# Two graph-attention layers on one core: the second group's score row through TensorE, and other places for steps of the prologue

## The chip, the core and the metric

The kernel runs on one core of a Trainium2 chip. The metric is the device time of one execution in microseconds (us), lower is better. Everything is 32-bit floating point, apart from the integer adjacency matrix.

The engines have short names in the profile: PE is TensorE's matrix multiply and PEld its weight load, DVE is VectorE, ACT is ScalarE, POOL is GpSimd, SP is SyncE, which here issues all DMA transfers.

## What is computed

`x` is 64 x 256 x 512 (64 graphs of 256 nodes), `adj` a 256 x 256 matrix of 0 and 1. Two layers follow each other, each with a layer norm and a ReLU ahead of it and a residual addition behind it:

```python
# layer 0: graph attention, W is 512 x 256
h = relu(layernorm(x)) @ W
e = leaky_relu(h @ a[0] + transpose(h @ a[1]), 0.2)      # 256 x 256 for each graph
out = softmax(where(adj, e, -1e9)) @ h
x = x + concat([out, h])
# layer 1: multi-head attention, 8 heads of 64, masked by adj
h = relu(layernorm(x))
q, k, v = h @ Wq.T + bq, h @ Wk.T + bk, h @ Wv.T + bv
x = x + softmax(where(adj, q @ k.T / 8, -inf)) @ v @ Wo.T + bo
```

## The kernel before

The 64 graphs are taken in 32 groups `g` of two graphs `b`; a graph has two tiles `t` of 128 nodes, so a group has four row tiles. The work of a group is written as Python generators, each cut into pieces by `yield`, and a hand-written order of letters says which piece comes when:

- `first_norm(g)` (letter n) is the layer norm ahead of layer 0. `measure(b)` takes statistics on VectorE, GpSimd makes the factor with a power, `norm(b)` writes `xn` on ScalarE, `turn(b)` transposes 32 x 32 blocks on VectorE into `xt` and sends them out (`passed<-xt`), `fetch(b)` brings them back with their blocks in other places (`moved<-passed`, four transfers), and `put(b)` copies them to the operand `hT0` on ScalarE. For the group 0 the turning is done on TensorE instead (`pt`).
- `first_layer(g)` (letter s; for the groups 0 and 1 in the prologue also 0 and 1) makes the features `H = ph`, the attention `e` and the sums `po`. The scores h @ a[0] and h @ a[1] are the first two columns of H. One of them must lie along a row in all partitions: that is the score row, `own`.
- `project(g)` (letter u in the prologue) makes q, k and v of layer 1 in seven products each (Strassen's scheme: sums of quarters of the operands and of the weights, in the order 1, 2, 6, 7, 5, 4, 3). The accumulator of the first product stays in a held bank of PSUM, and ScalarE copies intermediate states to `kept_q`, `kept_k`, `kept_v`. The seventh product of k in the group 0 uses the bank that q's first product held, so it has to wait for q's last copy (`q<-pq`) on ScalarE. From the group 2 on the features are made in the same way (`first_products`).
- `judge()` (letter c) and `mask()` (letter e) make, in the prologue only, bounds on the inputs and the transposed mask: `gram_q`, `gram_k`, then `square_q` and `square_k` in two rounds.
- `weight_sums(name)` makes four sums of the quarters of one weight matrix, on VectorE or GpSimd; `first_weight_sums()` does so for W (GpSimd); `last_bias()` multiplies bv into Wo (`bv_rows`, `pb`).
- `scores(g, b)` (letter S) makes `sc` and the exponentials `p`; `mask_pairs` (m) masks p on VectorE and adds halves on GpSimd; `fold` (f) sends p out (`rows<-p`) and back (`parts<-rows`), adds on GpSimd, and sums on VectorE (`compact<-parts`), which gives the softmax's denominators; `weigh` makes `pr` and `oT`, and `outputs` (o) makes `py`.

Score rows are made in two ways. For the group 0 TensorE transposes a broadcast column of H into PSUM (`pn`). For the others `score_rows(g)` transposes H's first columns on VectorE (`rows<-H`), writes a row of 2 KB to DRAM (`line<-rows`) and reads it back into all partitions (`own<-line`).

A scheduler sets the order of the instructions on each engine from the program's order and the dependencies. Where the kernel wants an order of its own it adds a dependency without a semaphore: `after(instruction, name)`, and `not_sooner(engine, ...)` for "not ahead of the last one that was recorded for this engine". TensorE is pinned throughout (`in_order`). Each engine works through its stream in order, and so does SyncE with the issues of transfers. The lists `put_last`, `norm_last` and others hold names of instructions that later ones are pinned behind.

Buffers that matter here: `xt`, `e` and `r` are single; `parts` of graph 0 takes the buffer of `e`, `own` that of `r`; `xn` and `moved` are double; `kept` is threefold; five banks of PSUM rotate (`mm`), three are held. The prologue of the kernel before ends with these lines (i counts the pieces of `project(0)` from 4 to 20):

```python
    take(*"uunuu0011cc")
    order = "nnn ssn n s - s ss ss s s n - n s - s -".split()
    for i, parts in enumerate(order, 4):
        next(products)
        ...
```

In the profile nearly all TensorE instructions have the line L137 (the helper that pins them; transposes L140) and the other engines' L35 (the helper that remembers the last instruction), so they are told apart by their tiles.

Of the kernel before, what the change touches and what calls it, by code (L numbers as in the profile page):

```python
# [57 lines left out]
def bounded(  # L58
# [56 lines left out]
    def after(instruction, name):  # L115

        tc.add_manual_dep(
            instruction.ins, name,
            mybir.DependencyInfo(mybir.DependencyClass.NoSync, mybir.DependencyReason.DATA),
            reason="the engine's order",  # L120
        )

    def not_sooner(engine, operation, *args, **kwargs):

        last = engine.last
        after(getattr(engine, operation)(*args, **kwargs), last)
# [126 lines left out]
    def weight_sums(name, engine=vector):  # L253
        w = w_sb[name]
        not_sooner(engine, "tensor_sub", w[:, :, T3, :], w[:, :, W22, :], w[:, :, W12, :])
        engine.tensor_sub(w[:, :, T1, :], w[:, :, W12, :], w[:, :, W11, :])
        engine.tensor_sub(w[:, :, T2, :], w[:, :, W22, :], w[:, :, T1, :])
        engine.tensor_sub(w[:, :, T4, :], w[:, :, W21, :], w[:, :, T2, :])
# [8 lines left out]
        not_sooner(gpsimd, "tensor_sub", t2, w22, w12)  # L267
        not_sooner(gpsimd, "tensor_sub", t4, w21, t2)

    put_last, norm_last, edge_last, sums_last, turn_last = [], [], [], [], []  # L270

    def last_bias():

# [346 lines left out]

    def score_rows(g):
        rows = small.tile([P, GT, 8], F32, tag="rows", name=f"rows_{g}", bufs=2)
        not_sooner(vector, "transpose", rows.rearrange("p t c -> p (t c)"), H[:, :, 0:8])
        line = dram.tile([P // 8, S], F32, tag="line", name=f"line_{g}")
        not_sooner(sync, "dma_start", line, rows.rearrange("p t c -> p (t c)")[::8, :])
        own = att.tile([P, P // S, GT, S], F32, tag="r", name=f"own_{g}", bufs=1)
        not_sooner(
            sync, "dma_start", own.rearrange("p k t j -> p (k t j)"),
            line.rearrange("(o k) j -> o (k j)", o=1).to_broadcast([P, TOK]),
        )  # L630
        return own.rearrange("p k t j -> p t k j")
# [64 lines left out]
    def first_layer(g):  # L696
# [38 lines left out]
        pT = {}  # L735
        if g > 1:
            own = owns.pop(g)
            yield
        elif g:
            own = score_rows(g)  # L740
            yield
        else:
            yield
            pn = mm(f"pn_{g}")
            for t in range(GT):
                transpose(pn[:, t * P : (t + 1) * P], H[:, t, 0:1].to_broadcast([P, P]), ident)
            own = pn.rearrange("p (t k j) -> p t k j", t=GT, j=S)
# [103 lines left out]
    def projection(g, name, ops):  # L851
        shape = [P, NT, D] if name == "v" else [P, HP, N]
        turn[0] = 1 - turn[0]
        firsts = 2 if (g, name) == (0, "k") else turn[0]
        sevenths = 1 - turn[0]

        def blocks(bank):
            return bank.rearrange("p (o n) -> p o n", o=2)

        def product(out, i, start):  # L860
            a, w = ops[i][0], w_sb[name][:, :, ops[i][1], :]
            for o in range(2):
                cols = slice(o * P, (o + 1) * P)
                for c in range(2):
                    of, by = (a[:, c, cols], w[:, c, :]) if name == "v" else (w[:, c, cols], a[:, c, :])
                    matmul(
                        out[:, o, :], of, by, start=start and o == c == 0, stop=o == c == 1,
                        skip_group_check=True,
                    )

        def part(b, half):
            if (name, g, b) not in qkv:
                qkv[name, g, b] = place(shape, f"{name}_{g}_{b}")
            to = qkv[name, g, b][0]
            if name == "v":
                return to[:, :, half * D // 2 : (half + 1) * D // 2]
            return to[:, 2 * half : 2 * half + 2, :]

        def take(to, bank, half):

            behind = [scalar.last] if g == 0 and name != "v" else []
            if name == "v":
                taken = [scalar.copy(to, bank)]
            else:
                taken = [
                    scalar.activation(
                        to[:, o, :], bank[:, o, :], AF.Identity,
                        bias=bcol[name][:, 2 * half + o : 2 * half + o + 1], scale=1.0,
                    )
                    for o in range(2)  # L890
                ]
            for last in behind:
                for instruction in taken:
                    after(instruction, last)

        def kept(bank, half, i):
            s = att.tile([P, 2, N], F32, tag="kept", name=f"kept{i}_{name}_{g}", bufs=3)
            take(s, bank, half)
            return s

        first = blocks(held_bank(firsts, f"p{name}1_{g}"))
        product(first, 1, True)
        p1 = kept(first, 0, 0)
        yield
        second = blocks(mm(f"p{name}2_{g}"))
        product(second, 2, True)
        vector.tensor_add(part(0, 0), second, p1)
        yield
        product(first, 6, False)
        p16 = kept(first, 0, 1)  # L910
        yield
        second = blocks(held_bank(sevenths, f"p{name}7_{g}"))
        product(second, 7, True)
        p7 = kept(second, 1, 2)
        yield
        product(first, 5, False)
        vector.tensor_add(part(1, 1), first, p7)
        yield
        product(second, 4, False)
        vector.tensor_add(part(1, 0), second, p16)  # L920
        yield
        product(first, 3, False)
        take(part(0, 1), first, 1)
        yield

# [54 lines left out]
    def fold(g, b, p):  # L980

        if g == NG - 1:
            return
        compact = small.tile([P, NQ, N // S], F32, tag="compact", name=f"compact_{g}_{b}", bufs=2)
        row_sums[g, b] = compact
        pool, tag, bufs = (att, "e", 1) if b == 0 else (big, "hT0", 2)
        rows = []

        def put(quad):
            rows.append(dram.tile([P, QH, N], F32, tag="rows", name=f"rows_{g}_{b}_{quad}"))
            heads = slice(quad * QH, (quad + 1) * QH)
            not_sooner(sync, "dma_start", rows[quad], p[:, heads, 0, :])

        def fetch(quad):
            parts = pool.tile([P, P // S, N], F32, tag=tag, name=f"parts_{g}_{b}_{quad}", bufs=bufs)
            for j in range(QH):
                not_sooner(
                    sync, "dma_start", parts[j * S : (j + 1) * S],  # L1000
                    rows[quad][:, j, :].rearrange("(i a) n -> a i n", a=S),
                )
            return parts

        def add(parts):
            not_sooner(gpsimd, "tensor_add", parts[:, :2], parts[:, :2], parts[:, 2:])
            not_sooner(gpsimd, "tensor_add", parts[:, 0], parts[:, 0], parts[:, 1])

        def sum_up(quad, parts):
            not_sooner(vector, "transpose", parts[:, 1], parts[:, 0])  # L1010
            vector.reduce_sum(
                compact[:, quad], parts[:, 1].rearrange("p (k a) -> p k a", a=S), axis=AX.X
            )

        put(0)
        parts = fetch(0)
        yield
        put(1)
        yield
        add(parts)  # L1020
        yield
        sum_up(0, parts)
        parts = fetch(1)
        yield
        add(parts)
        yield
        sum_up(1, parts)
        vector.reciprocal(compact, compact)
        yield
# [103 lines left out]
    def take(*names):  # L1133
        for name in names:
            next(work[name])
# [10 lines left out]
    take(*"n00c0n0n")  # L1146
    late_loads()
    weight_sums("q")
    take(*"uunuu0011cc")
    order = "nnn ssn n s - s ss ss s s n - n s - s -".split()  # L1150
    for i, parts in enumerate(order, 4):
        next(products)
        if i == 4:
            take("c")
        if i == 17:
            weight_sums("o", gpsimd)
        if i in (5, 12):
            weight_sums("kv"[i // 12])
        if i == 8 and NG > 3:
            load(3, 0)  # L1160
            load(3, 1)
        if i == 11:
            take(*"cc")
        if i == 7:
            first_weight_sums()
        for part in parts:
            if part != "-":
                next(norms if part == "n" else pieces, None)
        if i in (15, 19, 20):
            next(bias)  # L1170
    additions = (piece for g in range(NG) for piece in residual(g))

# [428 lines left out]
```

## Time and profile before

| | before |
|---|---|
| median of 3 runs | 2406.9 us (2406.54 to 2407.69) |
| the profiled execution: time | 2408.41 us |
| the profiled execution: span from first to last instruction | 2406.8 us |
| granted TensorE clock, mean over the span | 0.997 |
| instructions in the profile | 43080 |
| DMA traffic | 343.76 MB, mean 143 GB/s |

The page gives for each engine the time in which it was busy and its share of the span, then groups of instructions, written as what they write, an arrow to the left, and what they read (`ph<-w_sb,hT`), with a count and a mean duration. A timeline lists instructions in order of time: start, duration, engine, line, operation, tiles, shapes, count, and in brackets the idle time ahead of the instruction with what ended it. A 32-bit matmul appears as two records. A granted clock of 1.00 means TensorE at full speed.

### The profile page before, as it was taken

What the parts mean: (1) busy time and instruction counts of PE and PEld (TensorE: products, weight loads), DVE (VectorE), ACT (ScalarE), POOL (GpSimd) and SP (SyncE); (2) the same over time, 40 slices, a digit from 0 to 9 for tenths busy, and PEclk for the clock granted to TensorE, in tenths of its full rate; (3) what the DMA queues carried; (4) which work ended last, traced back from release to release, by engine and by line L of the source; (5) the groups of instructions that cost most, each with busy time, mean ns of one, the idle gap of its engine ahead of it and who ended that gap; (6) DMA issues with size and microseconds to landing.
All of it is one profiled execution on the core that took longest, in us unless ns stands there. A gap on an engine that the chain in (4) does not pass through costs nothing.

```text
span 2406.8 us, 43080 instructions
## 1 busy us (share of the span) xinstructions
PE 2386.7 (99%) x15824; PEld 2014.5 (84%) x15824; DVE 1687.7 (70%) x3346; ACT 1020.9 (42%) x2017; POOL 1420.4 (59%) x1290
## 2 busy tenths in 40 slices
PE   9899999999999999999999999999999999999999
PEld 8778888888888888888888888888888888888886
DVE  7576766777766767667767677776677676676665
ACT  4444444444444444434444444444344444343431
POOL 4456657566666556575556666565655566656552
PEclk9999999999999999999999999999999999999999
DMA  6344444544454444455444444444554445454331
GB/s 194 105 127 145 137 154 149 157 152 134 139 160 149 148 142 138 152 151 166 147 138 134 156 149 148 149 141 142 155 165 145 136 136 163 147 157 141 112 106 46
DMA packets 272041, 343.76 MB, mean 143 GB/s; under 512 B 25424, under 2 KB 217168, under 8 KB 271824
## 3 DMA queue, kind: packets, MB, share of 16 engines
q1 hardware_dynamic: 271824, 340.95, 45.5%
q8 instruction: 126, 2.06, 0.4%
q14 instruction: 91, 0.75, 0.1%
HBM read 177.22 MB, written 163.64 MB: 142 GB/s over the span
## 4 chain that ended last, share of the span: by engine, by line
PE 97%; DMA 1%; DVE 1%; ACT 0%; SPq 0%; issue 0%; POOL 0%; DVEq 0%; ACTq 0%
PE pq L137 16%; PE pk L137 16%; PE py L137 16%; PE pv L137 16%; PE sc L137 10%; PE pr L137 9%; PE ph L137 8%; PE po L137 5%; DMA adj_i<-in_adj_dram 0%; DMA wv_sb<-in_L_gnn_Wv_dram 0%; DMA line<-rows 0%; ACT e L35 0%; PE total L137 0%; PE gram_q L137 0%; PE gram_k L137 0%
## 5 line engine op out<-in xcount | busy, mean ns | idle before, releaser
L35 POOL TENSOR_TENSOR p<-p 128x512 f32<-128x512 f32 x248 | 384.5, 1563 | 490.0 <-DVE p L35 470.4
L35 ACT ACTIVATE xn<-x,factor 128x512 f32<-128x512 f32 x256 | 194.7, 807 | 328.2 <-POOL factor L35 319.3
L35 DVE TENSOR_TENSOR p<-p,maskT 128x1024 f32<-128x1024 f32 x254 | 323.4, 1294 | 2.0 <-ACT p L35 2.0
L35 DVE TENSOR_TENSOR x<-py,x 128x256 f32<-128x256 f32 x448 | 185.9, 415 | 192.8 <-PE py L137 186.5
L35 ACT ACTIVATE p<-sc 128x512 f32<-128x512 f32 x512 | 258.3, 627 | 144.0 <-PE sc L137 127.3
L35 POOL TENSOR_TENSOR parts<-parts 128x512 f32<-128x512 f32 x248 | 248.1, 1001 | 83.0 <-DMA parts<-rows 56.8
L137 PE MATMUL py<-wo_sb,oT 128*128 128x256 f32 x1024 | 262.4, 379 | 0.6 <-DVE oT L35 0.6
L137 PE MATMUL sc<-q,k 64*128 64x256 f32 x2048 | 253.5, 392 | 4.9 <-ACT p L35 4.9
L137 PEld LDWEIGHTS sc<-q,k 64*128 64x128 f32 x2048 | 205.9, 188 | 53.0 <-issue 26.3
L137 PE MATMUL pk<-hT,wk_sb 128*128 128x256 f32 x1024 | 245.6, 383 | 2.8 <-ACT q L35 2.8
L137 PE MATMUL pq<-hT,wq_sb 128*128 128x256 f32 x1024 | 240.0, 382 | 0.7 <-ACT hT L35 0.7
L137 PE MATMUL pv<-wv_sb,hT 128*128 128x256 f32 x1024 | 236.8, 379 | 0.0
L137 PE MATMUL pr<-p,v 128*32 128x256 f32 x4096 | 234.2, 380 | 0.0
L137 PEld LDWEIGHTS pq<-hT,wq_sb 128*128 128x128 f32 x1024 | 191.9, 190 | 36.0 <-issue 10.3
L137 PEld LDWEIGHTS pk<-hT,wk_sb 128*128 128x128 f32 x1024 | 189.9, 190 | 36.6 <-issue 9.9
L35 POOL TENSOR_TENSOR factor<-factor,rexp 128x2 f32<-128x2 f32 (+1 forms) x132 | 117.8, 892 | 171.4 <-DVE factor L35 171.1
L137 PEld LDWEIGHTS py<-wo_sb,oT 128*128 128x128 f32 x1024 | 194.2, 190 | 28.2 <-DVE oT L35 1.1
L137 PEld LDWEIGHTS pv<-wv_sb,hT 128*128 128x128 f32 x1024 | 194.6, 190 | 26.5
L137 PEld LDWEIGHTS pr<-p,v 128*32 128x32 f32 x4096 | 126.8, 110 | 97.8 <-issue 16.9
L137 PE MATMUL py<-wo_sb,o_sums 128*128 128x256 f32 x768 | 197.6, 380 | 0.5 <-DVE x L35 0.5
L137 PE MATMUL pv<-wv_sb,sums 128*128 128x256 f32 x768 | 181.6, 379 | 0.5 <-ACT kept_v L35 0.5
L137 PE MATMUL pk<-sums,wk_sb 128*128 128x256 f32 x768 | 181.5, 379 | 0.0
(150 smaller groups left out, 4076.2 us busy)
## 6 DMA issues: line engine op xcount, KB each, us to landing
passed<-xt SPq DMA_DIRECT2D x124, 512.0 KB, 3.1
moved<-passed SPq DMA_DIRECT2D x496, 128.0 KB, 3.4
rows<-p SPq DMA_DIRECT2D x124, 512.0 KB, 3.4
parts<-rows SPq DMA_DIRECT2D x496, 128.0 KB, 2.9
x<-in_x_dram SPq DMA_DIRECT2D x64, 512.0 KB, 4.3
out_dram<-x SPq DMA_DIRECT2D x62, 512.0 KB, 4.0
own<-line SPq DMA_DIRECT2D x31, 256.0 KB, 3.1
wq_sb<-in_L_gnn_Wq_dram SPq DMA_DIRECT2D x2, 512.0 KB, 9.1
```

Source lines behind the costliest of these rows:

```text
L35: instruction = getattr(self.engine, operation)(*args, **kwargs)
L137: in_order(nc.tensor.matmul(*args, **kwargs))
```

## The change

- The group 1 takes its score row as the group 0 does: TensorE transposes into `pn`, and `score_rows(1)`, with its VectorE transpose and its two transfers, is gone.
- The order of pieces in the prologue is another: the last operand copy of the group 1 (`hT0`) is taken ahead of the loop; the group 1's features, scores and products `po` come earlier among q's products; the third group's second norm and turn follow its first; the second round of squares comes at i = 6; the sums of wv come at i = 11 instead of 12, those of wo at i = 13 instead of 17, those of W after the pieces of i = 6 instead of ahead of those of i = 7; the bias begins at i = 12 instead of 15.
- In `take`, the copies of the group 1's q are pinned behind the last operand copy (`put_last`).
- In `score_rows(2)`, the transpose is pinned behind the last reduction of the fold (`fold_last`, a new list that `sum_up` sets).

```diff
-    put_last, norm_last, edge_last, sums_last, turn_last = [], [], [], [], []
+    put_last, norm_last, edge_last, sums_last, turn_last, fold_last = [], [], [], [], [], []
...
     def score_rows(g):
         rows = small.tile([P, GT, 8], F32, tag="rows", name=f"rows_{g}", bufs=2)
-        not_sooner(vector, "transpose", rows.rearrange("p t c -> p (t c)"), H[:, :, 0:8])
+        last = vector.last
+        turned = vector.transpose(rows.rearrange("p t c -> p (t c)"), H[:, :, 0:8])
+        for other in [last, *fold_last] if g == 2 else [last]:
+            after(turned, other)
...
         if g > 1:
             own = owns.pop(g)
-            yield
-        elif g:
-            own = score_rows(g)
             yield
         else:
             yield
...
             behind = [scalar.last] if g == 0 and name != "v" else []
+            if (g, name) == (1, "q"):
+                behind = list(put_last)
...
                 compact[:, quad], parts[:, 1].rearrange("p (k a) -> p k a", a=S), axis=AX.X
             )
+            fold_last[:] = [vector.last]
...
-    take(*"uunuu0011cc")
-    order = "nnn ssn n s - s ss ss s s n - n s - s -".split()
+    take(*"uunuu0011cccn")
+    order = "nn nsss nsn ssn ss - s s - - - - s - s - -".split()
     for i, parts in enumerate(order, 4):
         next(products)
-        if i == 4:
-            take("c")
-        if i == 17:
+        if i == 13:
             weight_sums("o", gpsimd)
-        if i in (5, 12):
-            weight_sums("kv"[i // 12])
+        if i in (5, 11):
+            weight_sums("kv"[i // 11])
         if i == 8 and NG > 3:
             load(3, 0)
             load(3, 1)
-        if i == 11:
-            take(*"cc")
-        if i == 7:
-            first_weight_sums()
         for part in parts:
             if part != "-":
                 next(norms if part == "n" else pieces, None)
-        if i in (15, 19, 20):
+        if i == 6:
+            take(*"cc")
+            first_weight_sums()
+        if i in (12, 19, 20):
             next(bias)
```

## The prediction

> **What bounds the kernel now.** I read the page first, then the windows over the first 180 us, then the waits of TensorE, then the timelines of TensorE, SyncE and VectorE around each long wait. The engine shares name the bound:
>
> ```profile
> PE 2386.7 (99%) x15824; PEld 2014.5 (84%) x15824; DVE 1687.7 (70%) x3346; ACT 1020.9 (42%) x2017; POOL 1420.4 (59%) x1290
> ```
>
> TensorE is idle for 20.1 of 2406.8 us. The windows (columns: length, busy time of PE, PEld, DVE, ACT, POOL, granted clock, DMA share, GB/s) show that this idle time lies in the prologue, and that the clock falls there too:
>
> ```profile
> 30.00:60.00 30.00, 28.59 (x151) 25.02 (x150) 21.93 (x48) 15.36 (x32) 16.03 (x22) 1.00 0.57 168
> 60.00:90.00 30.00, 26.63 (x119) 21.99 (x118) 21.51 (x42) 13.82 (x29) 8.24 (x8) 0.94 0.31 103
> 90.00:120.00 30.00, 27.15 (x159) 24.34 (x158) 12.47 (x18) 12.43 (x28) 20.73 (x16) 0.94 0.35 109
> 120.00:150.00 30.00, 25.10 (x167) 19.75 (x167) 20.10 (x39) 12.12 (x24) 14.39 (x13) 0.89 0.24 78
> 150.00:180.00 30.00, 30.00 (x201) 24.88 (x200) 23.98 (x48) 13.94 (x24) 20.07 (x20) 1.00 0.63 178
> ```
>
> From 150 us until close to the end TensorE has no gap, so a microsecond saved before 150 should arrive at the end whole. The waits of TensorE name three long ones:
>
> ```profile
> PE sc L137 <- ACT p L35: 4.9, 1, 4.9
> PE ph L137 <- POOL sums_xn L35: 2.8, 1, 2.8
> PE pk L137 <- ACT q L35: 2.8, 1, 2.8
> ```
>
> Each costs twice. In TensorE's timeline (start, duration, what) eight pq/pk records follow each other every 1.73 us, but the ones behind a long wait are stretched:
>
> ```profile
> 58.67 1.89 PE L137 MATMUL pk<-sums,wk_sb 128*128 128x256 f32 x8
> 63.38 2.71 PE L137 MATMUL pk<-hT,wk_sb 128*128 128x256 f32 x8 [2.83 <-ACT q L35]
> 65.88 2.91 PE L137 MATMUL po<-H,e 128*128 128x257 f32 x8
> 68.63 1.89 PE L137 MATMUL pk<-sums,wk_sb 128*128 128x256 f32 x8
> ```
>
> The pk at 63.38 wants q's held bank. Its take stands on ScalarE behind e of the second group (59.51), which waits for own<-line: rows at 54.09, line at 54.33, own at 56.07, landed at 59.5. The last wait has a queue as its cause. VectorE had the third group's rows ready at 118.47, but SyncE stood at the parts transfer, which waits for the fold's reduction (123.32 to 123.74), and only then issued the line (VectorE's timeline, then SyncE's):
>
> ```profile
> 118.26 0.21 DVE L35 STREAM_TRANSPOSE rows<-H 128x32 f32<-128x32 f32 x1
> ...
> 123.32 0.42 DVE L35 TENSOR_REDUCE compact<-parts 128x8 f32<-128x256 f32 x1
> ```
>
> ```profile
> 123.81 1.74 SPq L35 DMA_DIRECT2D parts<-rows  x4
> 125.59 0.54 SPq L35 DMA_DIRECT2D line<-rows  x1
> 128.43 0.35 SPq L35 DMA_DIRECT2D own<-line  x1
> ```
>
> **What the Trainium skill says.** "TensorE: Matmul & The Clock Gate", Part 1, says that the array falls to half clock after about 3.4 us idle, in a free-running window, and needs as long of work to come back. The trace agrees in kind: clock 0.67 in 63.4 to 68.6, 0.54 in 112.3 to 116, 0.57 in 135.6 to 140.3, each after a wait of 2.8 to 4.9 us; after waits of 0.5 to 0.7 us it stays 1.00. [...] here the 2 KB line takes 2.2 us in the median and own 3.4. "GPSIMD Engine Reference", Key points, says that GpSimd shares SBUF interfaces with VectorE, with contention where VectorE has two SBUF inputs; here a p mask takes 1.18 us alone and 2.30 beside GpSimd at 100.87. I keep such stretches at their measured length.
>
> **Stage A, up to the first sc (91.46 before).** *Removed:* one VectorE transpose (0.21), two SyncE issues (0.58 and 0.36), the 5.4 us from rows to own. *Added:* four transposes pn. The first group's took from 19.26 to 20.04, 0.78 us with the wait for the last H copy; the four of pt_mask without it 0.47. I take 0.78, bounds 0.45 to 1.0; TensorE runs in order, so four more instructions can't be a gain.
> - ScalarE now copies the squares and hT before kept_q. The second half of moved is issued at 43.01 to 44.7 and lands within 3.1 us, 47.4; hT's first copy ends at 48.0, ahead of TensorE's own time 49.06. ph starts there instead of 49.90: gain 0.84. kept_q, now behind hT, is wanted by VectorE only near 59.
> - ScalarE then has kept_q, kept_q, two xn of the third group (GpSimd's factor is ready at 50.56, so 50.6 to 52.1) and the H copies (to 53.1). pn ends near 53.3, and e runs 53.4 to 55.0 instead of 59.51 to 61.2.
> - VectorE: both leaky steps to 55.8, a q addition to 56.4, two xt transposes to 57.8 (1.29), masks at 58.5 and 59.2. TensorE meanwhile has pq 1.73, the squares 0.89 + 0.89, pq 1.73 and reaches po at 58.55: just no wait. The squares moved here are the cover; without them po would wait about 1.8 us.
> - q's take follows the third pq (62.2 to 63.0); pk wants it at 65.5. The wait of 2.98 us (60.40 to 63.38 by cadence) goes, and with it the slow stretch (5.25 us from 63.38 to 68.63 instead of 3.46): 1.79.
> - The moved second norm and turn take two ACTIVATE (1.52), two transposes (1.29) and one 512 KB transfer. On SyncE it passes the two x loads of the fourth group, which now wait until about 64.7 instead of 57.7; they land near 72 and are first read near 110. The single xt buffer makes the next transposes wait for the transfer (3.3 us): at worst some 0.4 us at the last pk. The two xn no longer stand between the kept_v copies (80.84 and 84.61), so pv's waits go (0.67 + 0.19 + 0.2 small ones): about 1.0.
> - Weight sums: those of wo and w0 keep their place in GpSimd's stream, those of wv are only split around a k addition. Nothing, covered by the pv products' 3.5 us head start on the third sum.
>
> Sum of A: 0.84 + 2.98 + 1.79 + 1.0 - 0.78 = **5.8 us**; first sc near 85.6.
>
> **Stage B, ph of the third group** (times from the first sc). The pin puts hT's copies ahead of the third kept_q. Before: hT's second copy ended at 18.1 and GpSimd's sums began at 18.2. Now the copies run 10.2 to 12.5 (transfer landed by 8.7), but GpSimd is still in the p additions until 16.5. So sums_xn is ready at 19.1 instead of 20.8, and hT's difference at 20.4. The price: kept_q ends at 13.3, and pq wanted it at 12.58, a new wait of 0.7. ph then waits 0.45 and 0.34. All three are short, so the clock should hold. The stretch from the first ph (107.50) to pk (118.52) was 11.02 us; its work is 6.2, so 4.8 were lost; 1.5 to 1.7 stay. Gain **3.1**: pk at 23.9 instead of 27.06.
>
> **Stage C, e and sc of the second half.** Now the fold's reduction stands ahead of rows. GpSimd's parts additions end near 23.9, the reduction at 24.9, rows at 25.6. SyncE issues four parts (1.74) and line at 26.7; own at 29.2, landed at 32.6 (before 40.5). Two more chains end at e: the second fold (GpSimd 29.9 to 31.9, VectorE to 33.0) and ScalarE's xn and kept_k (33.0). e starts at 33.0, and p 3.0 us later as before (131.94 to 134.94). TensorE reaches sc at 34.4, fills three banks by 35.6 and waits for p until 36.6: 1.0 instead of 4.9, too short to slow the clock. From pk to the next pk<-sums (118.52 to 140.33) it was 21.8 us; now 15.4. Gain **6.4**.
>
> **Sum.** 5.8 + 3.1 + 6.4 = 15.3. VectorE then follows TensorE about 2 us closer than before; py's second read of x had some 2.4 us of slack there. Cost 0 to 1.5, I take 0.8: **14.5 us**. The profiled execution took 2408.41 (span 2406.8), 1.5 above the median of 2406.9. From its own time the sum gives 2393.9, from the median 2392.4; I forecast the latter.
>
> **Rivals.**
> - *e is still late in stage C* (12%): three chains meet within 0.4 us; if one slips by 2 us, the wait is 3 again and the slow stretch of about 2.1 us returns. Gain 10 to 10.5: 2396.6. For it: the fold and own now cross the same SyncE queue. Against it: each piece has its measured length.
> - *Only the e wait of stage A goes* (8%): GpSimd sets stage B and SyncE sets stage C, and the pinned kept_q eats what is left. Gain 5 to 6: 2401.2.
> - *Slower* (3%): the main loop no longer absorbs VectorE's closer following. TensorE has no idle time over 30 groups of about 75 us; if each later group waited 0.65 us at py or po, 30 x 0.65 = 19.5 outweighs the gain and gives about 2412. It decides from 0.48 us a group. Against it: VectorE is idle 19 to 23 us in each such 75 us.
> - *The reorder does nothing* (2%): 2406.9. Against it: pn and the moved squares do stand in TensorE's stream.
>
> **The numbers.** 75% for the sum, with its bounds 2389.5 to 2396; the first rival reaches 2399. Range 2389.5 to 2399.0. About 0.2% (4.8 us) is what a measurement of this kernel can tell. Faster 0.93 (sum, first rival, nearly all of the second), within 0.04, slower 0.03.
>
> **What would show it.** In the new profile: pn near 52.5 with about 0.8 us; e of the second group near 53.5; no long wait before pk; clock 1.00 in the three windows; a wait of about 0.7 at pq and under 0.5 at ph; line issued right after parts, about 27 us after the first sc; sc waiting about 1 us; first sc near 85.6. A wait over 2.5 us anywhere before 150, or idle TensorE after it, proves me wrong.

## The result: 0.54% faster, and the profile after

The median of five runs is 2394.47 us (2394.21 to 2394.69), beside 2407.53 (2406.54 to 2408.81) for five runs of the kernel before: a ratio of 0.9946, 95% interval 0.9931 to 0.9960. The profiled execution took 2394.69, with a span of 2393.0 and a mean granted clock of 1.000. The forecast was 2392.4 with a range of 2389.5 to 2399.0: right in direction and within its range, 2.1 too low.

The page's engine shares first. TensorE is now idle for 2393.0 - 2381.7 = 11.3 us, beside 20.1 before, while its busy time fell too, by 5.0, mostly because the stretched records behind the three long waits are gone:

```profile
PE 2381.7 (100%) x15828; PEld 2010.1 (84%) x15828; DVE 1691.4 (71%) x3345; ACT 1021.8 (43%) x2017; POOL 1422.4 (59%) x1290
```

The windows (length, busy time of PE, PEld, DVE, ACT, POOL, granted clock, DMA share, GB/s): the clock stands at 1.00 in all of them, and TensorE is busy for about 10 us more between 60 and 150:

```profile
60.00:90.00 30.00, 30.00 (x152) 25.64 (x152) 21.56 (x42) 12.85 (x25) 7.73 (x8) 1.00 0.43 146
90.00:120.00 30.00, 29.03 (x204) 24.57 (x206) 13.64 (x25) 13.74 (x32) 27.75 (x23) 1.00 0.36 113
120.00:150.00 30.00, 29.52 (x158) 25.11 (x151) 26.45 (x58) 12.80 (x23) 15.45 (x16) 1.00 0.40 118
```

The waits of TensorE (total, count, longest): the pk wait has left the list, ph fell from 2.8 to 0.6, sc from 4.9 to 0.5, and the pinned kept_q has come in:

```profile
PE ph L137 <- POOL sums_xn L35: 0.6, 1, 0.6
PE py L137 <- DVE x L35: 0.5, 2, 0.3
PE sc L137 <- ACT p L35: 0.5, 1, 0.5
PE pq L137 <- ACT kept_q L35: 0.3, 1, 0.3
```

TensorE's timeline in stage A. The four pn take 0.79 up to the next pq (53.50), po and pk have no bracket, so they waited for nothing, and pk is back at 1.89 a record group, where it was 2.71 before:

```profile
52.71 0.95 PE L140 MATMUL pn<-ident,H 128*128 128x128 f32 x4
53.50 1.89 PE L137 MATMUL pq<-sums,wq_sb 128*128 128x256 f32 x8
...
58.84 2.00 PE L137 MATMUL po<-H,e 128*128 128x257 f32 x8
...
65.87 1.89 PE L137 MATMUL pk<-hT,wk_sb 128*128 128x256 f32 x8
```

The same view in stages B and C, from the first sc at 85.82 on: three waits, all short.

```profile
98.91 1.99 PE L137 MATMUL pq<-hT,wq_sb 128*128 128x256 f32 x8 [0.34 <-ACT kept_q L35]
...
104.98 1.16 PE L137 MATMUL ph<-w_more,sums_xn 128*128 128x129 f32 x8 [0.57 <-POOL sums_xn L35]
...
122.54 2.85 PE L137 MATMUL sc<-q,k 64*128 64x256 f32 x22 [0.48 <-ACT p L35]
```

SyncE's timeline: parts and line still follow each other at once, but 26.8 us after the first sc instead of 34.1.

```profile
110.83 1.73 SPq L35 DMA_DIRECT2D parts<-rows  x4
112.60 0.54 SPq L35 DMA_DIRECT2D line<-rows  x1
115.42 0.34 SPq L35 DMA_DIRECT2D own<-line  x1
```

For the rest I use a table of four marks, read from TensorE's timeline of each profile and counted from the first pq (32.44 before, 32.61 after), because the first 33 us scatter between executions by up to 1 us. *sc* is the first sc (end of stage A), *pk* the first pk of the third group (end of B), *pk2* the next pk<-sums behind the wait for e (end of C), *py* the last py.

| kernel | sc | pk | pk2 | py | median of its runs |
|---|---|---|---|---|---|
| before | 59.02 | 86.08 | 107.89 | 2368.40 | 2407.53 |
| after | 53.21 | 77.29 | 92.71 | 2353.66 | 2394.47 |
| after, second profile | 53.21 | 77.28 | 92.74 | 2353.64 | 2395.07 |
| without the q pin | 53.21 | 77.28 | 92.71 | 2353.42 | 2394.03 |
| without both pins | 53.28 | 77.38 | 96.29 | 2356.72 | 2397.65 |
| row by DMA | 57.84 | 82.05 | 97.41 | 2357.84 | 2398.76 |
| squares late | 55.72 | 79.73 | 94.92 | 2355.52 | 2396.60 |
| before + both pins | 57.37 | 81.43 | 97.16 | 2357.83 | 2398.89 |
| before + second pin | 58.81 | 84.57 | 106.44 | 2367.31 | 2408.45 |
| before + pn | 55.28 | 82.66 | 105.19 | 2365.85 | 2406.83 |
| sums at old places | 53.20 | 77.29 | 92.96 | 2353.64 | 2395.76 |
| half addition on VectorE | 53.21 | 76.51 | 94.97 | 2356.07 | 2397.36 |

The gains by stage are then 5.81 in A, 2.98 in B (24.08 from sc to pk instead of 27.06) and 6.39 in C (15.42 instead of 21.81), 15.18 in all.

### The profile page after: what moved, and what is told of

It is laid out like the page before. It is cut to its first block, busy times and chain, and to the rows that moved or that the text cites. A ratio compares the mean times of both kernels' runs of the same rounds, so it can differ in the third digit from the quotient of the medians.

```text
span 2393.0 us, 43082 instructions
## 1 busy us (share of the span) xinstructions
PE 2381.7 (100%) x15828; PEld 2010.1 (84%) x15828; DVE 1691.4 (71%) x3345; ACT 1021.8 (43%) x2017; POOL 1422.4 (59%) x1290
## 4 chain that ended last, share of the span: by engine, by line
PE 98%; DMA 1%; DVE 0%; ACT 0%; issue 0%; POOL 0%; SPq 0%; ACTq 0%; POOLq 0%; DVEq 0%
PE pq L137 16%; PE pv L137 16%; PE pk L137 16%; PE py L137 16%; PE sc L137 10%; PE pr L137 9%; PE ph L137 8%; PE po L137 5%; DMA adj_i<-in_adj_dram 0%; DMA wv_sb<-in_L_gnn_Wv_dram 0%; PE total L137 0%; PE gram_q L137 0%; PE gram_k L137 0%; ACT hT L35 0%; DMA parts<-rows 0%
## 5 line engine op out<-in xcount | busy, mean ns | idle before, releaser
L35 DVE TENSOR_TENSOR p<-p,maskT 128x1024 f32<-128x1024 f32 x254 | 328.4, 1313 | 3.2 <-ACT p L35 3.2
```

What stands on the lines that cost most here:

```text
L35: instruction = getattr(self.engine, operation)(*args, **kwargs)
```

## The experiments

Beside the experiments, 9 to 17 runs of the kernel before were taken on the same chip; their medians were 2409.30, 2408.49 and 2408.82.

### The score row: does pn carry stage A?

```diff
         if g > 1:
             own = owns.pop(g)
             yield
+        elif g:
+            own = score_rows(g)
+            yield
```

> The changed kernel, with the second group's score row made as before the change (VectorE transpose, row written out and read back) instead of four TensorE transposes. Theory (the row through TensorE is what brings e forward by 5 in stage A): e starts near 58.8 instead of 53.7, TensorE waits 3.5 to 4 at po or the pk behind it, and a slow-clock stretch of 1.8 follows; less 0.8 for the transposes: 4.5 to 5 slower, near 2399.2. Rival (the reordering alone gives the gain, the row has cover): no slower than 0.5, near 2395.

Measured 2398.76 (2396.61 to 2399.60), ratio to before 0.9957 (0.9944 to 0.9971). TensorE's timeline shows the wait where it was expected, and behind it the stretched po (3.61 for what takes 2.00):

```profile
61.97 3.61 PE L137 MATMUL po<-H,e 128*128 128x257 f32 x8 [3.75 <-DVE e L35]
```

So 4.63 of A's 5.81 fall away with the row (1.6 of it by the stretched po). In the new order the old row would have kept only 1.2 in stage A; B and C are untouched (24.21 and 15.36).

The other way round, pn alone in the kernel before (the diff is against that kernel):

```diff
-        elif g:
-            own = score_rows(g)
-            yield
```

> The kernel before with only the second group's row turned on TensorE; order of pieces, weight sums and pins as before. Theory (the row's 5.4 is what made e and q's take late): pk's wait of 2.8 and its slow stretch of 1.8 go, 0.8 is paid for the transposes, near 2403.5; ph still waits 2.8 and sc 4.9. Rival (the masks or q's take are held by something else on ScalarE or VectorE): pk still waits over 2, near 2407.

Measured 2406.83 (13 runs, 2403.94 to 2408.94), ratio 0.9991 (0.9983 to 1.0000). In TensorE's timeline pk's wait has shrunk to 0.32, nearly as the theory says, and stage A is 3.74 shorter. But of that only 2.55 are left at the last py, because stage B is 0.32 longer, sc waits longer (5.21 instead of 4.90) and its stretch is 0.41 longer (5.24 instead of 4.83):

```profile
62.03 1.99 PE L137 MATMUL pk<-hT,wk_sb 128*128 128x256 f32 x8 [0.32 <-ACT q L35]
...
133.18 5.24 PE L137 MATMUL sc<-q,k 64*128 64x256 f32 x22 [5.21 <-ACT p L35]
```

The rival's cause is refuted (pk does not wait over 2), though the time is the one that it named (near 2407). The theory's size was too large: the gain in the runs is about 2, not 4, and its interval reaches down to nothing. Here a stage's gain was not kept whole, since the waits behind it remained.

### The squares: are they the cover of po?

```diff
         if i == 6:
-            take(*"cc")
             first_weight_sums()
+        if i == 11:
+            take(*"cc")
```

> The changed kernel with the second round of squares back in its old place (i = 11), so that they no longer stand between the second group's features and po. Theory (the squares are the cover of the masks): TensorE reaches po 1.8 earlier, waits there 1.4 to 1.8 for the masked p, clock stays 1.00; the squares' time comes back later, so 1.4 to 1.8 slower, near 2396.1. Rival (VectorE runs its masks earlier when TensorE runs ahead, so cover is not needed): within 0.4 of the changed kernel, near 2394.5.

Measured 2396.60 (2396.17 to 2398.21), ratio 0.9951 (0.9937 to 0.9964), and 1.86 later at the last py. TensorE's timeline:

```profile
58.47 2.00 PE L137 MATMUL po<-H,e 128*128 128x257 f32 x8 [1.73 <-DVE e L35]
```

TensorE reached po two squares (1.78) sooner and stood there for 1.73: the masks did not come sooner. The squares are the cover, as the prediction said ("would wait about 1.8").

### The two pins

The first pin alone is enough to give all that both give: with the second one left out, the streams of all engines are the same, instruction for instruction, in the new order as well as in the old one. Without the first:

```diff
-            if (g, name) == (1, "q"):
-                behind = list(put_last)
```

> The changed kernel without the pin that holds the second group's q copies behind the last operand copy; ScalarE then runs its third kept_q between the two hT copies, all else stays. Theory (GpSimd's p additions, not ScalarE, set stage B; the pin only costs the wait at pq): pq no longer waits 0.34 for kept_q, ph still waits about 0.6 for sums_xn, about 0.4 faster than the changed kernel, near 2394.0. Rival (the pin is what brings hT ahead of GpSimd and so carries stage B): ph waits 2.8 again, the clock falls behind it, about 3 slower, near 2397.5.

Measured 2394.03 (2393.67 to 2395.10), ratio 0.9940 (0.9927 to 0.9954). pq's wait is gone, but TensorE then arrives at ph that much sooner and waits there for GpSimd, so that sc, pk and pk2 stand where they stood:

```profile
104.50 1.16 PE L137 MATMUL ph<-w_more,sums_xn 128*128 128x129 f32 x8 [1.16 <-POOL sums_xn L35]
```

The rival falls. The median is 0.44 lower, but these marks have not moved and the changed kernel's own two medians differ by 0.6, so the theory's 0.4 is not shown: the wait only moved. GpSimd, which adds p until then, sets stage B. Without both:

```diff
-            if (g, name) == (1, "q"):
-                behind = list(put_last)
...
-        for other in [last, *fold_last] if g == 2 else [last]:
-            after(turned, other)
+        after(turned, last)
```

> The changed kernel without both pins (second group's q copies, third group's rows behind the fold's reduction). VectorE then makes rows before the reduction, as before the change, with two BN_STATS between. Theory (stage C's gain comes from the earlier work of stage A and B that lets rows, reduction and GpSimd's sums come close together; the pins only set the order of two neighbours): the line is issued 1 to 2 later, sc waits 1.5 to 2 instead of 0.48, 1 to 1.5 slower than the changed kernel, near 2395.5. Rival (the pins carry stage C): sc waits 4 to 5 again and the clock falls behind it, 6.4 slower, near 2401.

Measured 2397.65 (2395.85 to 2401.83), ratio 0.9955 (0.9942 to 0.9969). Stage B keeps its gain (24.10); stage C takes 18.91 instead of 15.42. SyncE issues the line 28.6 us after the first sc (1.8 later), because VectorE's reduction ends 1.8 later, and TensorE waits 2.29. The line came as the theory said and the wait a little longer, but the kernel was about 3 slower than the changed one and not 1 to 1.5: the theory left out that the clock falls behind such a wait (4.54 instead of 2.85). The five runs spread over 6 us. SyncE's timeline, then TensorE's:

```profile
114.36 0.54 SPq L35 DMA_DIRECT2D line<-rows  x1
```

```profile
124.33 4.54 PE L137 MATMUL sc<-q,k 64*128 64x256 f32 x22 [2.29 <-ACT p L35]
```

Both pins in the kernel before, whose row, order and weight sums are kept (the diff is against that kernel):

```diff
...
-        not_sooner(vector, "transpose", rows.rearrange("p t c -> p (t c)"), H[:, :, 0:8])
+        last = vector.last
+        turned = vector.transpose(rows.rearrange("p t c -> p (t c)"), H[:, :, 0:8])
+        for other in [last, *fold_last] if g == 2 else [last]:
+            after(turned, other)
...
+            if (g, name) == (1, "q"):
+                behind = list(put_last)
...
+            fold_last[:] = [vector.last]
```

> The kernel before with the two pins alone (second group's q copies behind the last operand copy, third group's rows behind the fold's reduction); row by DMA, order of pieces and weight sums as before. Theory (stages B and C of the prediction are the pins' work, stage A is the order's and the row's): gain of 3.1 + 6.4, near 2398.0, with the pk wait of 2.8 near 63 still there and the waits at ph and sc under 1. Rival (without the earlier stage A the pins only change neighbours; B and C stay GpSimd's and SyncE's): within 1 of before, near 2407.

Measured 2398.89 (2398.10 to 2399.99), ratio 0.9963 (0.9949 to 0.9976). Stage B takes 24.06 (gain 3.0) and C 15.73 (gain 6.1): the pins alone, and so the first pin alone, bring what the prediction gave to B and C. Stage A was also 1.65 shorter than in the kernel before, though nothing differs there; that is the clock, below. The second pin alone in the kernel before:

```diff
-            if (g, name) == (1, "q"):
-                behind = list(put_last)
```

This diff is against the last kernel.

> The kernel before with the second pin alone (third group's rows behind the fold's reduction). Beside the kernel with both pins (2398.89, ph waiting 0.5 and sc 0.8) it parts the two stages: ScalarE's third kept_q and the q take stand ahead of the hT copies again, VectorE's reduction stands ahead of rows but behind the k addition. Theory (the q pin is stage B, the order of reduction and rows is stage C, each by itself): ph waits 2.8 again and pk stays 27.1 after the first sc; the line is issued 1 to 2 later than with both pins, sc waits 1.5 to 3, so some 3 to 4 of the 9 remain: near 2404. Rival (stage C's gain needs the earlier stage B): sc waits over 4.5 and the time stays within 1.5 of before, near 2407.5.

Measured 2408.45 (13 runs), ratio 0.9997 (0.9989 to 1.0005): nothing. The theory's half on stage B holds (ph waits 2.8; pk stands 25.8 after the first sc and not 27.1, since the clock did not fall behind this wait). Its half on C falls: the line comes 32.8 after the first sc (34.1 before), sc waits 5.1. VectorE's timeline shows why: the reduction does stand ahead of rows, but behind a k addition that waits 4.02 for TensorE:

```profile
120.61 0.69 DVE L35 TENSOR_TENSOR k<-pk,kept_k 128x512 f32<-128x512 f32 x1 [4.02 <-PE pk L137]
121.21 0.43 DVE L35 STREAM_TRANSPOSE parts<-parts 128x256 f32<-128x256 f32 x1
121.68 0.42 DVE L35 TENSOR_REDUCE compact<-parts 128x8 f32<-128x256 f32 x1
122.02 0.20 DVE L35 STREAM_TRANSPOSE rows<-H 128x32 f32<-128x32 f32 x1
```

The rival's outcome came: in the old order, stage C's gain needs the pin that shortens stage B. Since that pin moves the reduction too, the run does not tell whether C needs the shorter B or only the earlier reduction.

### The weight sums, and what limits stages B and C now

```diff
-        if i == 13:
+        if i == 17:
             weight_sums("o", gpsimd)
-        if i in (5, 11):
-            weight_sums("kv"[i // 11])
+        if i in (5, 12):
+            weight_sums("kv"[i // 12])
...
-        if i in (12, 19, 20):
+        if i in (15, 19, 20):
             next(bias)
```

> The changed kernel with the weight sums of wv (i = 12), wo (i = 17) and the bias (i = 15) at their places of before. Theory (these moves cost and bring nothing): within 0.4 of the changed kernel, near 2394.5. Rival (they clear VectorE for stage A): pv waits for its sums of wv or e's masks come later, 1 or more slower, near 2396.

Measured 2395.76 (2394.18 to 2397.26), ratio 0.9950 (0.9936 to 0.9963); the median is 1.3 above the changed kernel's, outside the theory's 0.4 and near the rival's number. But in the profile (an execution of 2394.18) no pv and no po waits, the first sc stands within 0.01 and the last py within 0.02 of the changed kernel's; only stage C is 0.25 longer. So neither of the rival's causes is there, and the five runs spread over 3.1: these moves bring nothing that the profile shows, and the 1.3 stays unexplained.

To see whether GpSimd's p additions are the last limit, one of the four went to VectorE, with the first pin left out:

```diff
...
-    def mask_pairs(p, last_group):
+    def mask_pairs(p, last_group, first):
...
-            last = gpsimd.last
-            made = gpsimd.tensor_add(pair[:, :, 0, :], pair[:, :, 0, :], pair[:, :, 1, :])
+            adder = vector if first and i == HP - 1 else gpsimd
+            last = adder.last
+            made = adder.tensor_add(pair[:, :, 0, :], pair[:, :, 0, :], pair[:, :, 1, :])
...
-                    masks = mask_pairs(waiting[2], g == NG - 1)
+                    masks = mask_pairs(waiting[2], g == NG - 1, g == b == 0)
```

> The changed kernel without the pin on q's copies and with one of the four half additions of p (first graph, last pair) on VectorE instead of GpSimd. Theory (GpSimd's p additions set the remaining wait of ph): sums_xn comes about 1.3 sooner, ph's wait of 0.57 and pq's of 0.34 go, and the fold's additions, line and e follow sooner so that sc's 0.48 goes too: 0.9 to 1.4 faster than the changed kernel, near 2393.2. Rival (VectorE's own work then delays the fold's reduction and rows): sc waits 1 or more, no faster, near 2395.

Measured 2397.36 (2395.07 to 2398.45), ratio 0.9953 (0.9940 to 0.9967): 2 to 3 slower than the changed kernel. Stage B is 0.78 shorter, but C 3.04 longer, of which 1.69 is the stretched sc. Of GpSimd's additions the first, beside VectorE's mask, takes about 2.25 in both kernels and one that runs alone 1.27; the second ran beside VectorE's new addition and took 1.72 instead of 1.27. So rows<-p left 14.55 after the first sc instead of 14.10, and GpSimd then stood waiting for parts to land, 1.64 instead of 0.37. Timelines of GpSimd and TensorE:

```profile
108.33 2.07 POOL L35 TENSOR_TENSOR parts<-parts 128x512 f32<-128x512 f32 x2 [1.64 <-DMA parts<-rows]
```

```profile
123.21 4.54 PE L137 MATMUL sc<-q,k 64*128 64x256 f32 x22 [1.83 <-ACT p L35]
```

The rival's outcome came (sc waits over 1), by another way than it said: not VectorE's own queue, but the chain of rows, parts, reduction and line. In this kernel that chain sets stage C; what is gained ahead of it in TensorE only lengthens sc's wait.

### The scatter of the times

> The changed kernel once more, beside runs of the kernel before on the chip of the experiment above. Theory (its short waits leave the clock alone, so its time does not scatter, while that of the kernel before goes with the number of slow-clock stretches that an execution happens to have): 2394 to 2395.5 with a spread under 2, granted clock 0.999 or 1.000 in each run; before 2406 to 2411 with 0.996 to 0.998. Rival (the scatter is the chip's or the day's): the changed kernel spreads over 3 too.

Measured 2395.07 (2394.13 to 2395.59), ratio 0.9939 (0.9925 to 0.9952): spread 1.5. The 17 runs of the kernel before beside it lie between 2406.56 and 2412.23, a little wider than expected; those with a mean granted clock of 0.998 are at 2406.6 to 2408.3, those with 0.996 at 2410.6 to 2412.2. So most of the scatter of one program, about 5 us, goes with the amount of slow clock that it happens to have. Short waits don't end this altogether: the kernel with the weight sums at their old places, whose waits are as short, spread over 3.1.

## Why the prediction was right, point by point

- **The bound and the three waits** stood: all of the gain lies between 33 and 125 us, and no wait over 1.1 is left in TensorE's list. Not all of the idle time lay in the prologue, though: of the 20.1 us, 14.1 lay ahead of 150 us and 5.5 in the last 16.8 us.
- **Stage A** was 5.81 for 5.8. ph came 0.84 sooner (16.62 after the first pq instead of 17.46), pn took 0.79 (0.78), po waited for nothing, pk for nothing, q's take began at 62.61 (62.2), pv's waits are gone. The two experiments on the row and the one on the squares show the cause of the largest terms, pk's and po's. The gains at ph and pv belong to the order: both stay where the row goes by DMA, and with pn alone ph waits 0.68 and pv 0.52 as before. Which of its moves makes them was not shown.
- **Stage B** was 2.98 for 3.1. The new wait at pq was over-sized: 0.34, not 0.7. ph waited 0.57, not 0.45; the second wait of 0.34 has no bracket, but the step from the first to the second of these ph (104.98 to 106.20) is 1.22 where later ones are 0.89 to 1.00. The prediction's cause was half of it: in the new order the pin is not needed for B, as the run without both shows; hT's last copy ends 13.0 after the first sc there (18.1 before), ahead of the end of GpSimd's p additions (16.5). Which move of the new order brings it forward was not shown. In the old order the pin is what makes B.
- **Stage C** was 6.39 for 6.4: line 26.78 after the first sc (26.7), sc resumed at 36.72 (36.6). The wait in between was 0.48, not 1.0, since TensorE itself came 0.3 later (34.68 for 34.4). The prediction read the pin on rows as what moves the reduction. The runs show that in the new order either pin does so, and in the old one only the pin on q's copies.
- **The weight sums** cost nothing, as costed.
- **VectorE following closer**, 0.8, is not seen as such. From pk2 to the last py it is 2260.51 before and 2260.95 and 2260.90 in the two profiles after, but the nine experiments lie between 2260.4 and 2261.1 as well. The tail behind the last py is another 0.8 of the profiled difference: 5.96 before, 6.73 after, and from 5.95 to 6.82 over all profiles, so scatter too.
- **Two readings were narrower than they sound.** The 2.2 and 3.4 us for line and own are medians of two transfers in the first stretch; over the whole trace they are 2.7 and 3.1. And the mask ahead of the one at 100.87, at 99.74, ran beside GpSimd too and took 1.13, while GpSimd's addition then took 2.33: of the two that meet, one kept its length and the other grew.
- **The rivals.** None came: e is not late, stages B and C moved, the main loop did not pay.
- **Part of the agreement by stage is luck.** By the clocks that the prediction read, (1 - 0.67) x 5.2 + (1 - 0.54) x 3.7 + (1 - 0.57) x 4.7 = 5.4 of the 15.2 us are slow clock of that one execution. The run with both pins lost none of its share in A, with the same instructions.
- **The step that was off** is the last one, from the sum to the forecast. The stages summed to 15.3 and gave 15.2, worked out in an execution that took 2408.41; its own time less the sum and its cost was 2393.9 in the prediction, 0.8 below what was measured (2394.69). But I subtracted the same sum from the median of three runs, 2406.9, and forecast 2392.4. Those three were low: of the 43 runs of the kernel before beside the experiments only 6 took 2406.9 or less, and their median is 2408.7. An execution that is faster because it has less slow clock also has less of it to lose, so it saves less; that fits the mean clocks above, but no run shows it apart.

## What to carry to other kernels

Where a gain consists partly of slow-clock stretches, subtract it from the time of the execution in which they were measured, not from a median of others, and a median of three says little where times scatter by 5 us. Before a wait is taken away, name the chain that ends next behind it and its slack: here a wait at pq moved to ph whole, and what was gained ahead of ph came back at sc with interest. An order that a scheduler makes can be had from more than one pin, so take out each alone before crediting it.

## What the runs showed of the clock

The prediction expected a slow stretch behind every wait of about 2.8 us and none behind one under 1. The second half held; the first did not. Up to 66 us the kernel before and the one with both pins run the same instructions, and both wait for q's take. Windows from 63 to 69, first of the kernel before, then with both pins:

```profile
63.00:69.00 6.00, 5.62 (x18) 4.64 (x19) 1.35 (x4) 1.90 (x5) 0.00 (x0) 0.72 0.05 18
```

```profile
63.00:69.00 6.00, 5.33 (x25) 4.70 (x26) 2.73 (x8) 2.19 (x6) 0.00 (x0) 1.00 0.11 40
```

One execution lost 1.7 us of clock, the other none. The wait of 2.85 at ph shows the same, first in the kernel before, then in the one with the second pin alone:

```profile
112.29 2.09 PE L137 MATMUL ph<-w_more,sums_xn 128*128 128x129 f32 x8 [2.85 <-POOL sums_xn L35]
```

```profile
111.96 1.16 PE L137 MATMUL ph<-w_more,sums_xn 128*128 128x129 f32 x8 [2.85 <-POOL sums_xn L35]
```

That the stretch is missing in the second shows in the lengths: 1.16 for 2.09. A wait of 1.83 (the half addition) was followed by 0.72 over 122 to 128, while one of 1.73 (squares late) left the clock at 1.00. "TensorE: Matmul & The Clock Gate", Part 1, has the activity window (about 3.4 us) free-running, so that the same kernel meets it differently each time: the runs agree. That a wait has to fill such a window, as its table may be read, does not fit: 1.83 and 2.29 us of waiting were enough here. Both stand behind pr and sc, which the trace lists with 128*32 and 64*128 instead of 128*128; whether that counts is open, and behind the others the shortest wait with a slow stretch is 2.83. One window at half clock would lose 3.4 / 2 = 1.7 us by that page (an estimate), and 1.7 is what 0.72 over 6 us comes to.
